# The middle stage of a two-FFN and attention layer: from three interleaved generators to slots written by hand over four rounds, with sums made by accumulating DMAs

## The chip, the cores and the metric

The kernel runs on one NeuronCore of a Trainium2 chip. A core has TensorE (PE, matrix products), VectorE (DVE), ScalarE (ACT), GpSimd (POOL) and SyncE (SP), each with an instruction queue of its own that is worked off in order, and 16 DMA engines. The metric is the device time of one execution in microseconds (us); lower is better. PEld is PE's loading of weights, which runs beside its products.

## The reference

Eight batches of 1024 tokens with 256 features pass a macaron layer: half a feed-forward network (FFN), attention, half a feed-forward network, each added to its input.

```python
x = x + 0.5 * _L0_ffn_ref(_layernorm(x), ...)
x = x + _L0_attn_ref(_layernorm(x), w_qkv, w_proj, b_proj)
x = x + 0.5 * _L0_ffn_ref(_layernorm(x), ...)
```

The FFN is a mixture of experts. A softmax over 16 expert scores per token, with a bias, picks the best two of four groups of experts and then the best two experts (`_gate`); their outputs, `silu(x We1 + be1) * (x We3 + be3)` times `We2` plus `be2`, are weighted and added. A shared FFN of width 256 is added for all tokens. The attention is linear, with 16 heads of width 16: q and k pass a ReLU, `context = sum over tokens of v k`, and the result is `context q / (q . sum of k)`, projected with `w_proj`, plus `b_proj`.

## The kernel before

Tokens lie on the 128 partitions, 8 tokens of a batch on each, so x of a batch is a tile of 128 x 8 x 256 numbers (1 MB). All numbers are fp32 but for some small masks. There are five parts in order of time.

1. *First FFN, routing* (to about 230 us). For each batch: layer norm, transposes on PE, the shared FFN (`shared_units`, L756), and `route` (L275): gate scores on PE, some 45 small DVE operations for the choice, then ranks within each expert by three small products, and 16 scatters of 128 rows each from POOL (L428), which put each token's row twice into the buffer `xs_d`, sorted by expert.
2. *First FFN, experts* (`blocks`, L573, to about 528 us): blocks of 256 rows of one expert; the results are scattered by POOL into `ys_d` (L698), two rows per token. This part's order is written out by hand (`tc.manual_schedule()`).
3. *The middle stage* (523 to 1011 us): the first FFN's expert outputs are added to x, then attention, then the second FFN's layer norm and routing. This is what changes.
4. *Second FFN, experts*: `blocks` again, to about 1288 us.
5. The shared FFN of the other batches, the expert outputs, and the stores of the result.

In the middle stage three generators run one batch apart from each other, in rounds: `begin(r)`, `attention(r - 1)` and `finish(r - 2)` (L974 to L1008). `run` (L902) takes a step of each in turn, and so writes the instructions down. The order on each engine is then made by the scheduler, which may move an instruction of one generator past those of another. What each does for its batch:

- `begin`: `combine` (L793) loads the expert outputs in eight pieces of 256 KB (SP, L798) and adds each to x on DVE (L799); `layernorm` (L209): statistics of eight 256-wide rows on DVE (L216, L217), square root on ACT (L221), two small DVE steps (L222, L224), eight scaled rows on ACT (L231); `transposed` (L238): 128 x 128 transposes on PE (L244) and copies out of PSUM on ACT (L247).
- `attention` (L805): the bias is added to x on DVE (L811); then for each of the eight token tiles j the product pk for k and q (L821), their ReLUs on ACT (L825, L826), and the product pgs of the normed x with k, added up in PSUM over all j (L829); the sum of k on DVE (L834). When all tokens are through: pks (L841), its copy ksb (L845), gsum (L848); q is scaled by its denominator on DVE (L855 to L864); the context pcx, masked to the heads (L873, L877); pm and its copy mm (L881, L882); q's transposes; and the products pp, added to x on DVE (L889, L893).
- `finish`: layer norm and transposes for the second FFN, a store of x (L983) and of the transposed x (L985) for five of the batches, and `route`. For the other three batches (5, 6, 7), x and the transposed x stay in SBUF, and their shared FFN runs as further work in the stage's last rounds. Batch 7's shared FFN of the first FFN runs in round 0.

PSUM tiles of one tag share two buffers: p1 (pk), p3 (pgs), y (pks, pm, pp) and m (all transposes, gate scores, ranks). Of the SBUF tags, x has four buffers of 1 MB, xn eight half batches, xnT six, k two.

Of the kernel before, what the change touches and what calls it, by code (L numbers as in the profile page):

```python
# [19 lines left out]
P = 128  # L20
# [6 lines left out]
def macaron_kernel(  # L27
# [108 lines left out]
    bpj = const.tile([P, D], F32, name="bpj")  # L136
    nc.sync.dma_start(out=bpj[:], in_=b_proj.partition_broadcast(P))
# [6 lines left out]
    def load_late_weights():  # L144
        for g in range(4):
            es = slice(g * E // 4, (g + 1) * E // 4)
            nc.sync.dma_start(out=wall[:, es, :], in_=wexp[:, es, :])
        nc.sync.dma_start(out=wqk_sb[:], in_=w_qkT.rearrange("(c p) f -> p c f", p=P))
        nc.sync.dma_start(out=wv_sb[:], in_=w_v.rearrange("(c p) f -> p c f", p=P))
        nc.sync.dma_start(out=wproj_sb[:], in_=w_projT.rearrange("(c p) f -> p c f", p=P))  # L150

# [56 lines left out]

    def layernorm(xt, name, res, width, parts=1):  # L209

        n = NT // parts
        for part in range(parts):
            mv = rp.tile([P, n, 2], F32, tag="mv", name=f"mv_{name}_{part}", bufs=2)
            for t in range(n):
                st = rp.tile([P, 6], F32, tag="st", name=f"st_{name}_{part}_{t}", bufs=4)
                nc.vector.bn_stats(out=st[:], in_=xt[:, part * n + t, :])  # L216
                nc.vector.bn_aggr(out=mv[:, t, :], in_=st[:])  # L217
                if t % 2:
                    yield
            rstd = rp.tile([P, n], F32, tag="rstd", name=f"rstd_{name}_{part}", bufs=2)  # L220
            nc.scalar.activation(rstd[:], mv[:, :, 1], AF.Sqrt, bias=eps_ln[:])  # L221
            nc.vector.reciprocal(rstd[:], rstd[:])  # L222
            nmr = rp.tile([P, n], F32, tag="nmr", name=f"nmr_{name}_{part}", bufs=2)
            nc.vector.scalar_tensor_tensor(  # L224
                nmr[:], mv[:, :, 0], -1.0, rstd[:], ALU.mult, ALU.mult
            )
            for i in range(n):
                h, t = divmod(part * n + i, HT)
                if t == 0:
                    res.append(half("xn", [P, HT, width], f"xn_{name}_{h}"))  # L230
                nc.scalar.activation(  # L231
                    res[h][:, t, 0:D], xt[:, part * n + i, :], AF.Identity,
                    bias=nmr[:, i : i + 1], scale=rstd[:, i : i + 1],
                )
                if t == HT - 1:
                    yield

    def transposed(xns, name, res):  # L238
        for nb, xn in enumerate(xns):
            xnT = half("xnT", [P, NC, TB], f"xnT_{name}_{nb}")  # L240
            for c in range(NC):
                pt = ps_m.tile([P, TPB, P], F32, tag="m", name=f"pt_{name}_{nb}_{c}")
                for t in range(TPB):
                    nc.tensor.transpose(  # L244
                        pt[:, t, :], xn[:, t, c * P : (c + 1) * P], ident[:]
                    )
                nc.scalar.copy(xnT[:, c, :], pt.rearrange("p t n -> p (t n)"))  # L247
            res.append(xnT)
            yield
# [25 lines left out]
    def route(base, which, b, xns, xnT, fine=False):  # L275
# [28 lines left out]
        nc.scalar.activation(pr[:], pr[:], AF.Exp)  # L304
        nc.vector.tensor_reduce(sm[:], pr[:], axis=AX.X, op=ALU.add)
# [487 lines left out]
    def combine(which, b, xt):  # L793

        for j in range(0, NT, 2):
            for k in range(K):
                y = mid.tile([P, 2, D], F32, tag="u1", name=f"y_{which}_{b}_{j}_{k}", bufs=4)
# [7 lines left out]
    def attention(b, xt, axn, axnT):  # L805
        kh, qh = [], []
        ks = mid.tile([P, NB, D], F32, tag="u3", name=f"ks_{b}", bufs=4)
        pgs = [
            ps_h.tile([P, D], F32, tag="p3", name=f"pgs_{b}_{c}") for c in range(NC)
        ]  # L810
        nc.vector.tensor_tensor(  # L811
            xt[:], xt[:], bpj[:].unsqueeze(1).to_broadcast([P, NT, D]), ALU.add
        )
        for j in range(NT):
            nb, t = divmod(j, HT)
            if t == 0:
                kh.append(half("k", [P, HT, D], f"k_{b}_{nb}"))
                qh.append(half("xn", [P, HT, D], f"q_{b}_{nb}"))
            pk = ps_h.tile([P, 2, D], F32, tag="p1", name=f"pk_{b}_{j}")
            for c in range(NC):  # L820
                nc.tensor.matmul(  # L821
                    pk.rearrange("p k d -> p (k d)"), tile_of(axnT, c, j), wqk_sb[:, c, :],
                    start=(c == 0), stop=(c == NC - 1),
                )
            nc.scalar.activation(kh[nb][:, t, :], pk[:, 1, :], AF.Relu)  # L825
            nc.scalar.activation(qh[nb][:, t, :], pk[:, 0, :], AF.Relu)  # L826

            for c in range(NC):
                nc.tensor.matmul(  # L829
                    pgs[c][:], axn[nb][:, t, c * P : (c + 1) * P], kh[nb][:, t, :],  # L830
                    start=(j == 0), stop=(j == NT - 1),
                )
            if t == HT - 1:
                nc.vector.tensor_reduce(  # L834
                    ks[:, nb, :], kh[nb].rearrange("p j d -> p d j"), axis=AX.X, op=ALU.add
                )
            yield

        pks = ps_y.tile([P, D], F32, tag="y", name=f"pks_{b}")
        for nb in range(NB):  # L840
            nc.tensor.matmul(  # L841
                pks[:], ones[:], ks[:, nb, :], start=(nb == 0), stop=(nb == NB - 1)
            )
        ksb = mid.tile([P, D], F32, tag="b2c", name=f"ksb_{b}", bufs=4)
        nc.scalar.copy(ksb[:], pks[:])  # L845
        gs = big.tile([P, NC, D], F32, tag="wc", name=f"gsum_{b}", bufs=3)
        for c in range(NC):
            nc.scalar.copy(gs[:, c, :], pgs[c][:])  # L848
        yield

        qT = []
        for nb in range(NB):
            den = rp.tile([P, HT, H], F32, tag="den", name=f"den_{b}_{nb}", bufs=1)
            qk = half("k", [P, HT, D], f"qk_{b}_{nb}")
            nc.vector.tensor_tensor(  # L855
                qk[:], qh[nb][:], ksb[:].unsqueeze(1).to_broadcast([P, HT, D]), ALU.mult
            )
            nc.vector.tensor_reduce(
                den[:], qk.rearrange("p j (h d) -> p j h d", d=HD), axis=AX.X, op=ALU.add
            )  # L860
            nc.vector.tensor_scalar(den[:], den[:], ATTN_EPS, None, ALU.add)
            nc.vector.reciprocal(den[:], den[:])
            qv = qh[nb].rearrange("p j (h d) -> p j h d", d=HD)
            nc.vector.tensor_tensor(  # L864
                qv, qv, den[:].unsqueeze(3).to_broadcast([P, HT, H, HD]), ALU.mult
            )
            yield

        cm = mid.tile([P, NC, P], F32, tag="hb", name=f"cm_{b}", bufs=3)
        for c2 in range(NC):  # L870
            pcx = ps_h.tile([P, P], F32, tag="p3", name=f"pcx_{b}_{c2}")
            for c in range(NC):
                nc.tensor.matmul(  # L873
                    pcx[:], wv_sb[:, c, c2 * P : (c2 + 1) * P],
                    gs[:, c, c2 * P : (c2 + 1) * P], start=(c == 0), stop=(c == NC - 1),
                )
            nc.vector.tensor_tensor(cm[:, c2, :], pcx[:], mask2d, ALU.mult)  # L877
# [224 lines left out]
```

## Time and profile before

| | us |
|---|---|
| median of 6 runs | 1416.37 (1411.22 to 1423.46) |
| the profiled execution | 1413.6 |
| its span, first to last instruction | 1411.9 |
| PE busy in the span | 1192.7 (84%) |
| DVE busy | 875.6 (62%) |
| ACT busy | 624.3 (44%) |
| POOL busy | 580.7 (41%) |
| the parts before the stage, 0 to 513: PE busy | 426.0 |
| the middle stage, 523 to 1011.5: PE busy | 425.1 |
| the parts behind it, 1011.5 to 1411.9: PE busy | 339.3 |

The profile is of one execution. An engine is busy while one of its instructions runs; for a group of instructions the page gives the busy time, the mean length of one, and the idle time just before them with what released it. The granted clock is the share of TensorE's full clock that it was given.

### The profile page before, as it was taken

What the parts mean: (1) busy time and instruction counts of PE and PEld (TensorE: products, weight loads), DVE (VectorE), ACT (ScalarE), POOL (GpSimd) and SP (SyncE); (2) the same over time, 40 slices, a digit from 0 to 9 for tenths busy, and PEclk for the clock granted to TensorE, in tenths of its full rate; (3) what the DMA queues carried; (4) which work ended last, traced back from release to release, by engine and by line L of the source; (5) the groups of instructions that cost most, each with busy time, mean ns of one, the idle gap of its engine ahead of it and who ended that gap; (6) DMA issues with size and microseconds to landing.
All of it is one profiled execution on the core that took longest, in us unless ns stands there. A gap on an engine that the chain in (4) does not pass through costs nothing.

```text
span 1411.9 us, 20820 instructions
## 1 busy us (share of the span) xinstructions
PE 1192.7 (84%) x5696; PEld 850.9 (60%) x5696; DVE 875.6 (62%) x2496; ACT 624.3 (44%) x1332; POOL 580.7 (41%) x688
## 2 busy tenths in 40 slices
PE   7898876977888778997977878999988889896898
PEld 3555444866777654664644645666666678773455
DVE  6787655854445537775866856738775444553666
ACT  6665322443456544464454454444344446561110
POOL 1576645566655440004044144233357665552000
PEclk9999987999999989999989999899999999998999
DMA  9344313567678876434254131010357667787896
GB/s 352 128 168 169 117 63 118 161 189 204 203 182 242 214 203 190 138 130 157 74 174 163 55 121 51 31 43 35 109 179 210 198 202 211 208 205 223 281 308 211
DMA packets 123318, 233.71 MB, mean 166 GB/s; under 512 B 20405, under 2 KB 71354, under 8 KB 118208
## 3 DMA queue, kind: packets, MB, share of 16 engines
q1 hardware_dynamic: 97664, 164.15, 40.4%
q0 software_dynamic: 25536, 68.20, 12.7%
q8 instruction: 48, 0.79, 0.2%
q14 instruction: 70, 0.57, 0.1%
HBM read 132.25 MB, written 102.64 MB: 166 GB/s over the span
## 4 chain that ended last, share of the span: by engine, by line
PE 36%; DVE 21%; issue 14%; DMA 13%; ACT 6%; POOL 5%; SPq 3%; another core or an unknown queue 2%; POOLq 0%; DVEq 0%; ACTq 0%
PE q L668 8%; PE py_s L783 5%; PE p_s L768 5%; DMA y<-ys_d 4%; POOL ys_d L698 3%; PE qy L686 3%; DMA ys_d<-yo,at 3%; PE pk L821 3%; DMA b2c<-in_be_dram 2%; PE pp L889 2%; DVE st_f L216 2%; PE pxg L647 2%; PE pt_f L244 2%; PE pgs L829 2%
## 5 line engine op out<-in xcount | busy, mean ns | idle before, releaser
L698 POOL DMA_INDIRECT ys_d<-yo,at x276 | 282.1, 1022 | 251.3 <-DVE yo L694 164.3
L668 PE MATMUL q<-xgT,wc 128*128 128x128 f32 (+1 forms) x1568 | 285.7, 333 | 59.1 <-ACT xgT L652 54.8
L428 POOL DMA_INDIRECT xs_d<-xn_f,rowi x256 | 264.8, 1034 | 107.0 <-issue 58.9
L668 PEld LDWEIGHTS q<-xgT,wc 128*128 128x128 f32 x1568 | 235.2, 199 | 83.8 <-ACT xgT L652 64.0
L691 ACT ACTIVATE yo<-qy,at 128x256 f32<-128x256 f32 x276 | 116.6, 478 | 157.2 <-PE qy L686 48.7
L768 PE MATMUL p_s<-xnT_f,ws_sb 128*128 128x512 f32 x352 | 168.5, 618 | 7.8 <-ACTq L752 6.7
L783 PE MATMUL py_s<-ws_sb,hs_s 128*128 128x256 f32 x512 | 137.0, 408 | 28.5 <-DVE hs_s L774 20.8
L694 DVE SCALAR_TENSOR_TENSOR yo<-b2c,at,yo 128x256 f32<-128x256 f32 x276 | 121.3, 478 | 63.9 <-ACT yo L691 31.8
L675 DVE SCALAR_TENSOR_TENSOR hb<-q,wc,hb 128x128 f32<-128x128 f32 (+1 forms) x196 | 73.4, 399 | 131.1 <-PE q L668 51.6
L686 PE MATMUL qy<-wall,hb 128*128 x552 | 147.4, 390 | 1.4 <-PE qy L686 0.9
L783 PEld LDWEIGHTS py_s<-ws_sb,hs_s 128*128 128x128 f32 x512 | 98.5, 202 | 74.9 <-DVE hs_s L774 35.0
L773 ACT ACTIVATE hs_s<-p_s,bc 128x512 f32<-128x512 f32 x64 | 43.8, 687 | 198.1 <-PE p_s L768 153.4
L821 PE MATMUL pk<-wqk_sb,xnT_a 128*128 128x512 f32 x256 | 128.2, 624 | 0.0
L422 POOL TENSOR_SCALAR xn_f<-cw 128x4 f32<-128x4 f32 x64 | 17.7, 283 | 252.0 <-DVE cw L394 249.1
L686 PEld LDWEIGHTS qy<-wall,hb 128*128 128x128 f32 x552 | 104.5, 198 | 16.2 <-issue 2.1
L768 PEld LDWEIGHTS p_s<-xnT_f,ws_sb 128*128 128x128 f32 x352 | 68.0, 198 | 74.0 <-issue 60.9
L647 PE MATMUL pxg<-ident,xg 128*128 128x128 f32 x552 | 87.2, 279 | 24.2 <-DMA xg<-xs_d 22.7
L652 ACT COPY xgT<-pxg 128x512 f32<-128x512 f32 x138 | 82.2, 596 | 57.3 <-PE pxg L647 32.7
L674 ACT ACTIVATE hb<-q,wc 128x128 f32<-128x128 f32 (+1 forms) x196 | 76.3, 426 | 63.9 <-PE q L668 28.8
L647 PEld LDWEIGHTS pxg<-ident,xg 128*128 128x128 f32 x552 | 68.8, 144 | 45.3 <-DMA xg<-xs_d 14.9
L799 DVE TENSOR_TENSOR x<-x,y 128x512 f32<-128x512 f32 x104 | 69.1, 685 | 40.6 <-DMA y<-ys_d 23.3
L829 PE MATMUL pgs<-k,xn_a 128*128 128x256 f32 x256 | 69.8, 391 | 11.8 <-issue 8.8
(292 smaller groups left out, 1709.7 us busy)
## 6 DMA issues: line engine op xcount, KB each, us to landing
y<-ys_d SPq DMA_DIRECT2D x128, 256.0 KB
b2c<-in_be_dram SPq DMA_DIRECT2D x196, 128.0 KB
xg<-xs_d SPq DMA_DIRECT2D x80, 264.0 KB
xg<-xs_d SPq DMA_DIRECT2D x116, 132.0 KB
x<-xk SPq DMA_DIRECT2D x10, 1024.0 KB
xk<-x SPq DMA_DIRECT2D x9, 1024.0 KB
out_dram<-x SPq DMA_DIRECT2D x7, 1024.0 KB
wall<-in_wexp_dram SPq DMA_DIRECT2D x4, 1540.0 KB
```

Of the source, the lines that this page charges most:

```text
L428: nc.gpsimd.indirect_dma_start(out=v[:, :], out_offset=bass.IndirectOffsetOnAxis(ap=rowi[:, j, k : k + 1], axis=0), in_=xn[:, t, :], in_of ...
L647: nc.tensor.transpose(pt[:, c, s * P : (s + 1) * P], xg[i][:, s, c * P : (c + 1) * P], ident[:],)
L652: nc.scalar.copy(xgT[i][:], pt[:])
L668: nc.tensor.matmul(pt_[:, cs], w[:, s, o + c * P : o + (c + 1) * P], t[:, c, cs], start=(c == 0), stop=(c == NC - 1),)
L686: nc.tensor.matmul(py[:, s : s + 1, :], h[:, s * P : (s + 1) * P], w2s[s % len(w2s)], start=True, stop=True,)
L691: nc.scalar.activation(yo[:, s, :], py[:, s, :], AF.Copy, scale=a[:, s, 1:2])
L694: nc.vector.scalar_tensor_tensor(yo[:, s, :], b2[:, s % b2.shape[1], :], a[:, s, 1:2], yo[:, s, :], ALU.mult, ALU.add,)
L698: nc.gpsimd.indirect_dma_start(out=ys_views[i * NR + s][:, :], out_offset=bass.IndirectOffsetOnAxis(ap=a[:, s, 0:1].bitcast(I32), axis=0), ...
L768: nc.tensor.matmul(pt[:], w[:, c, s * P : (s + 1) * P], xnT[nb][:, c, :], start=(c == 0), stop=(c == NC - 1),)
L783: nc.tensor.matmul(py[:, t - t0, :], hs[s][:, t * P : (t + 1) * P], ws2_sb[:, s, :], start=(s == 0), stop=(s == NS - 1),)
L821: nc.tensor.matmul(pk.rearrange("p k d -> p (k d)"), tile_of(axnT, c, j), wqk_sb[:, c, :], start=(c == 0), stop=(c == NC - 1),)
L829: nc.tensor.matmul(pgs[c][:], axn[nb][:, t, c * P : (c + 1) * P], kh[nb][:, t, :], start=(j == 0), stop=(j == NT - 1),)
```

## The change

The first and last two parts stay as they are, but for a bias: `b_proj` is no longer kept in SBUF, but written eight times in a row into a buffer in DRAM, `bpj_d`, at the start.

In the middle stage:

- `combine` no longer adds the first FFN's expert outputs. `add_outputs` issues, from POOL, DMAs that add the outputs in DRAM to x in SBUF (`accum_op`), 1 MB each, two per batch; for batch 0 in two halves. `add_rows` adds the bias in the same way. (The last part of the kernel still uses `combine`.)
- The order of the stage is written by hand (`tc.manual_schedule()`): eleven rounds of eight slots, in which four batches are in work at once. In round r, batch g = r gets its first layer norm (slots 3 to 7), a = r - 1 the products over its tokens (one j per slot), p = r - 2 the rest of its attention (slots 0 to 6), and f = r - 3 the second layer norm's rows, transposes and the start of its routing (slots 0 to 3).
- The routing's further steps are spread by a table (`PLAN`; `SOON` for batch 6, `PART` for batch 7) over the slots up to slot 6 of the next round. `route` now gives way after the exponential too, and after each scatter.
- `layernorm`, `transposed` and `attention` become classes and functions whose pieces can be called one by one. q is kept in four tiles of two token tiles each, in other buffers (tags u1 and u3), and its scaling works on these 512-wide tiles in place of 1024-wide ones. qk uses tag u2 and not k, and pcx tag y and not p3.
- The shared FFN of batches 5 and 6 takes one step per slot in rounds 9 and 10 (rounds 8 and 9 before), batch 7's follows alone, as before. Round 0 is filled in the same way.

```diff
-    bpj = const.tile([P, D], F32, name="bpj")
-    nc.sync.dma_start(out=bpj[:], in_=b_proj.partition_broadcast(P))
+    bpj_d = tc.dram_tile([NT, D], F32, name="bpj_d")
...
+        nc.sync.dma_start(out=bpj_d[:, :], in_=b_proj.partition_broadcast(NT))
...
+    class Norm:
+        def stats(self, t):
+            st = rp.tile([P, 6], F32, tag="st", name=f"st_{self.name}_{t}", bufs=4)
+            nc.vector.bn_stats(out=st[:], in_=self.xt[:, self.first + t, :])
+            nc.vector.bn_aggr(out=self.mv[:, t, :], in_=st[:])
+        def scale(self):
...
+            nc.scalar.activation(self.rstd[:], mv[:, :, 1], AF.Sqrt, bias=eps_ln[:])
+            nc.vector.reciprocal(self.rstd[:], self.rstd[:])
...
+        def row(self, i):
...
+            nc.scalar.activation(
+                self.rows_[h][:, t, 0:D], self.xt[:, self.first + i, :], AF.Identity,
+                bias=self.nmr[:, i : i + 1], scale=self.rstd[:, i : i + 1],
+            )
...
         nc.scalar.activation(pr[:], pr[:], AF.Exp)
+        if fine:
+            yield
...
+    def add_outputs(b, xt, parts=1):
+        n = NT // parts
+        for k in range(K):
+            for i in range(parts):
+                js = slice(i * n, (i + 1) * n)
+                nc.gpsimd.dma_start(
+                    out=xt[:, js, :], in_=ys_v[k, b, :, js, :], accum_op=ALU.add
+                )
+    def add_rows(xt, src):
+        nc.gpsimd.dma_start(
+            out=xt.rearrange("p j d -> p (j d)"),
+            in_=src.rearrange("j d -> (j d)").partition_broadcast(P), accum_op=ALU.add,
+        )
...
+        def scale_q(self, nb):
...
+            for i, q in enumerate(pairs):
+                qk = mid.tile([P, 2, D], F32, tag="u2", name=f"qk_{b}_{nb}_{i}", bufs=3)
+                nc.vector.tensor_tensor(
+                    qk[:], q[:], self.ksb[:].unsqueeze(1).to_broadcast([P, 2, D]), ALU.mult
+                )
...
-    for r in range(B + 2):
-        if 2 <= r + 1 < B - 1:
-            xs[r + 1] = load_x(r + 1, xk_d[r + 1])
-        s = r - 3
-        run(
-            finish(r - 2) if r >= 2 else None,
-            attention(r - 1, xs[r - 1], *axns.pop(r - 1)) if 1 <= r <= B else None,
-            begin(r) if r < B else None,
-            late if r == 0 else None,
-            shared_units(xs[s], xnTs.pop(s), f"s1_{s}") if s >= B - LATE else None,
-        )
...
+    PLAN = {0: 1, 2: 2, 3: 2, 4: 1, 5: 1, 6: 1, 7: 1, 8: 4, 9: 4, 10: 4, 11: 4}
+    SOON = {0: 1, 1: 2, 2: 2, 3: 2, 5: 2, 6: 4, 7: 4, 8: 4, 9: 4}
+    PART = {0: 1, 1: 1, 2: 1}
...
+    def plan(r, b):
+        steps = PART if b == B - 1 else SOON if b == B - 2 else PLAN
+        for o, n in steps.items():
+            planned.setdefault((r + (3 + o) // 8, (3 + o) % 8), []).append((b, n))
...
+    def slot(r, s):
+        g, a, p, f = r, r - 1, r - 2, r - 3
+        G, A, Q, F = (0 <= b < B for b in (g, a, p, f))
+        if A:
+            att[a].products(s)
+            if s > 0:
+                att[a].over_tokens(s - 1)
+        if s == 0:
+            if Q:
+                att[p].over_tokens(NT - 1)
+                att[p].sum_k(1)
+                att[p].sums()
+            if A:
+                turn_half(axn[a], 1, f"a{a}", axnT[a])
+                add_rows(xs[a], bpj_d)
+            if F:
+                norm_f[f].stats(6)
+                norm_f[f].stats(7)
+                norm_f[f].scale()
+                norm_f[f].row(0)
+                norm_f[f].row(1)
+                if f < B - LATE:
+                    nc.sync.dma_start(out=xk_d[f][:], in_=xs[f][:])
+        elif s == 1:
+            if Q:
+                att[p].context()
...
+            if Q:
+                att[p].scale_q(0)
+            if F:
+                turn_half(xns[f], 0, f"f1_{f}", xnTs[f])
+        elif s == 2:
+            if Q:
+                att[p].project()
...
+            if Q:
+                att[p].scale_q(1)
+                att[p].turn_q(0)
+            if F:
+                turn_half(xns[f], 1, f"f1_{f}", xnTs[f])
+        elif s == 3:
+            if F:
...
+                routes[f] = route(base, 1, f, xns.pop(f), xnTs[f], True)
+                plan(r, f)
+            if Q:
+                att[p].turn_q(1)
+            if 2 <= r + 1 < B:
+                xs[r + 1] = load_x(r + 1, xk_d[r + 1])
+            if G:
+                norm_a[g] = Norm(xs[g], 0, NT, f"a{g}", axn.setdefault(g, []), D)
+                for t in range(4):
+                    norm_a[g].stats(t)
+            if Q:
+                att[p].add(0)
+        elif s == 4:
...
+            if A:
+                att[a].sum_k(0)
...
+            if Q:
+                att[p].add(2)
+            if 2 <= r + 1 < B:
+                add_outputs(r + 1, xs[r + 1])
+        elif s == 5:
+            if Q:
+                att[p].add(4)
+            if G:
+                norm_a[g].stats(6)
+                norm_a[g].stats(7)
+                norm_a[g].scale()
...
+        elif s == 6:
+            if Q:
+                att[p].add(6)
+            if G:
+                for i in range(4):
+                    norm_a[g].row(i)
...
+        elif s == 7:
+            if G:
+                for i in range(4, 8):
+                    norm_a[g].row(i)
+                axnT[g] = []
+                turn_half(axn[g], 0, f"a{g}", axnT[g])
...
+        for b, n in planned.pop((r, s), ()):
+            steps_of(routes[b], n)
+        if (r, s) == (B + 2, 3):
+            first.extend(first_map(base, 1))
+    with tc.manual_schedule():
+        add_outputs(0, xs[0], 2)
+        add_outputs(1, xs[1])
+        for r in range(B + 3):
...
+            for i in range(8):
+                slot(r, i)
+                if filler is not None:
+                    next(filler, None)
```

## The prediction, on record before the changed kernel ran

> **What bounds the kernel now.** I read the page's 40 slices first (35.3 us each; the middle stage is slices 16 to 29, counted from 1), then the middle stage cut at the starts of its rounds, then that stage's waits and groups, and last single instructions in order of time.
>
> ```profile
> PE   7898876977888778997977878999988889896898
> DVE  6787655854445537775866856738775444553666
> PEclk9999987999999989999989999899999999998999
> ```
>
> TensorE (PE) is the fullest engine in the stage, VectorE (DVE) second; in slices 21 to 25 PE stands at 7 or 8 tenths and DVE at 5 to 8, so neither is full there. The cut gives the size (columns: stretch, length, busy time of each engine, granted clock, DMA share, GB/s):
>
> ```profile
> 523.00:557.50 34.50, 28.96 (x74) 15.54 (x75) 22.19 (x52) 10.56 (x17) 4.34 (x5) 0.82 0.54 169
> ...
> 713.00:767.00 54.00, 43.52 (x202) 28.95 (x201) 37.61 (x103) 25.49 (x59) 18.20 (x26) 0.91 0.42 141
> ...
> 949.50:1011.50 62.00, 59.02 (x253) 36.94 (x254) 46.22 (x121) 24.27 (x38) 20.57 (x24) 1.00 0.17 55
> 523.00:1011.50 488.50, 425.09 (x1835) 274.60 (x1836) 335.94 (x854) 218.18 (x463) 132.77 (x174) 0.94 0.31 104
> ```
>
> The stage takes 488.5 us, PE is busy for 425.1 of them, and **63.4 us of PE idle time is all that a new order can win**. About 41 of it lies between 659 and 871: a full round there takes 54 us and PE works 43.5. The end (949.5 on) is nearly full already. Those holes are chains through in-order queues (waiter, what it waited for, total, times, longest; 505 to 1010 us):
>
> ```profile
> DVE rstd_a L222 <- ACT rstd_a L221: 27.4, 6, 7.1
> DVE x L799 <- DMA x<-xk: 17.0, 4, 8.2
> DVE ks L834 <- ACT k L825: 15.9, 3, 7.5
> ```
>
> One hole, as instructions (start, length, engine, line, idle before and its releaser):
>
> ```profile
> 759.44 0.59 PE L841 MATMUL pks<-ks,ones 128*128 128x256 f32 x2
> 764.62 2.17 PE L244 MATMUL pt_f<-ident,xn_f 128*128 128x128 f32 x8 [4.58 <-issue]
> ```
>
> PE stands for 4.58 us until the last batch's sums on DVE, square root and rows on ScalarE (ACT) are through: every batch ends in such a tail, and little else is ready.
>
> **Part 1: the outputs and the bias leave DVE.** Groups of the stage:
>
> ```profile
> L799 DVE TENSOR_TENSOR x<-x,y 128x512 f32<-128x512 f32 x48 | 31.7, 683 | 20.2 <-DMA x<-xk 17.0 <-DMA y<-ys_d 3.1
> L811 DVE TENSOR_TENSOR x<-x,bpj 128x2048 f32<-128x2048 f32 x6 | 13.7, 2278 | 0.0
> ```
>
> Eight adds of 0.68 and one of 2.28 go per batch: 7.7 us of DVE's 37.6 per round. The hand order gives some back: the query scaling becomes six 512-wide operations for three 1024-wide, twice (about 0.2 us each pair more), and routing steps now stand one behind the other, each on the one before (0.33 us from start to start at 752, against 0.20 when mixed with others). I put DVE at 33 us a round: no bound, but long chains.
>
> In their place POOL issues three accumulating DMAs per batch (four halves for batch 0): about 1 us each by the scatters' 1.03 (L428), so 3 more on its 18 of 54. The second add of a tile waits for the first to land, and the first for the load of x; behind them on POOL stand 12 scatters of the routing, and who waits for those is only the ring of eight xn tiles, two rounds later. Hidden in a full round: the load is issued in slot 3, x is wanted one round later. SP loses 64 loads of y, at which it stood for up to 20.3 us waiting for DVE (L798, the queue's own waits); the loads of x behind them go sooner, and the 17.0 us of DVE waits on them shown above go.
>
> The trace has no accumulating DMA. Low end: a plain load of x, issued 768.30, used 774.74: 6.4 us per MB. High end: that row doubled, 12.8, since the add reads x too. I take 8: the best slice of this trace's DMA moves 381 GB/s, 2.75 us per MB, doubled is 5.5, and 2.4 for landing (a scatter at 978.22 took 2.44). [...]
>
> **Part 2: the rounds.** PE's work is unchanged. Per batch, from start to start in the rows (two records per matmul): pk 32 x 0.43 = 13.8; pgs and pp 32 x 0.215 = 6.9 each; three sets of transposes 3.45 each = 10.4; pks, pcx, pm 0.86 each = 2.6; gate and ranks 1.9. Sum 42.5. A shared unit: 32 x 0.43 + 32 x 0.215 = 20.6. 8 x 42.5 + 4 x 20.6 = 422, against 425.1 busy. What the new order adds is where PE waits in a full round. I followed the four queues by hand from the end of the third product pair (pp of j=4, slot 5; call it 0):
>
> - *pk of slot 0.* ACT must pass: add and two statistics on DVE 1.7, root 0.3, reciprocal, next statistics and the softmax's start on DVE 2.1, exponential 0.3, then k/q 0.66, four rows 2.0, k/q 0.66, four rows 2.0, two copies 1.05: 10.8. PE has pg 0.4, two pk, two pgs, pp and transposes until then: 9.0. **Wait 1.8 to 2.3.**
> - *pks, slot 0.* DVE after the exponential (4.75): softmax 0.8, add 0.6, statistics 1.1, scores and groups 3.3, statistics 1.1, first pick 1.95, sum of k 1.9: done at 15.5. PE is there at 14.0 to 14.5. **Wait 1 to 1.5.**
> - *first transposes of xn_f, slot 1.* After pks, ACT: copies 0.6, table load 1.28, root 0.3, DVE 0.5, rows and k/q 2.7: 5.4 behind the transposes of slot 0; PE has 3.5. **Wait 1.5 to 1.9.**
> - *second transposes of xn_f, slot 2.* Both PSUM buffers of tag m are in use until ACT has copied the queries: **0.6**.
>
> 5.5 us, and about 0.1 for each of a dozen hand-overs: **6.8. Full round 42.5 + 6.8 = 49.3**, against 54.
>
> **Sum of the stage** (PE work plus waits):
> - round 0: the shared unit runs from 523. y can be read at 530.3 (the last scatter of the blocks lands); issue 1, data 5.5 for each add, one landing 2.4: both adds end near 544.5; statistics, root, rows, transposes and copy 7.5 more: pk starts at 551.5, against 557.5. **28.5**
> - round 1: 23.3 + 2.7 = **26**; round 2 with the context phase: 37.2 + 2.8 = **40**; round 3, without an older routing: **47**; rounds 4 to 7: 4 x 49.3 = **197**
> - round 8: 40.8 + 4.2 = **45**; round 9, shared unit 5 as filler: 39.8 + 3.2 = **43**; round 10, unit 6 and the block list on DVE (some 8 us, partly covered): 26 + 4 = **30**; the last unit alone: 20.6 + 2.4 = **23**
>
> 479.5 against 488.5: 9 less. So the gain per full round (4 to 5 us, five times) is mostly spent on a pipeline that is one stage deeper and on a last unit without company, which stood among other work in the old end. The stages before and after keep their instructions and order. The profiled execution took 1413.6 (span 1411.9 and 1.7 around it): 1413.6 - 9 = 1404.6, I say **1405**. The median of the runs shown is 1416.4, 2.8 above that execution; I keep the execution's base and leave the 2.8 to the range. The measurement can tell about 0.5%, 7 us, from no change.
>
> **The rivals.**
> - *The full round is tighter.* If pp of j=4 ends while DVE is already through its older work, as it is in my walk, small shifts pay: with the softmax's steps 2 us earlier the first two waits go, and 44 a round is left: 5 x 5 us less, **1380**. For it: 917 to 949.5 ran with 0.2 us of PE idle. Against: that stretch had an independent shared unit as filler, a full round has none.
> - *The full round is as long as the old ones.* Waits that my walk doesn't have come on top, as the ACT wait at 776.83 (3.31 us, releaser unknown to the profile), and in a hand order nothing else may step in: 52 a round, 5 x 2.7 = 13 more, **1418**. Then the change only shifts idle time.
> - *Slower: the accumulating DMA costs 12.8 us per MB.* Place: rounds 0 to 2, where it isn't hidden. Batch 0's two adds end near 557, pk starts at 564.5 (+13); batch 1's end at 583 where 575 is wanted (+8); the bias add and batch 2's end at 621 where 615 is wanted (+6): 1405 + 27 = **1432**. In later rounds 3 x 12.8 = 38 still fits in 49. It makes the kernel slower by over 0.5% from about 11 us per MB.
> - *It doesn't do what it says*: the built order has the slots as written on every queue, so I give this nothing.
>
> **How the numbers follow.** Forecast (1397 to 1411) 0.38; tighter rounds (1374 to 1396) 0.22; as long as before (1412 to 1421) 0.16; slow accumulation (1422 to 1436) 0.18; beyond either end 0.06. The range 1376 to 1434 takes in both ends of the DMA's price. Faster by over 0.5% (under 1407 to 1409): 0.28 of the forecast's 0.38, all of the tighter case and 0.02 beyond: 0.52. Same: 0.10 of the forecast, 0.13 of the third case: 0.23. Slower: the rest of it 0.03, the slow accumulation 0.18, 0.04 beyond: 0.25.
>
> **What would show it.** pk of batch 0 starting near 551 (DMA price); pk of successive batches 49 us apart in rounds 4 to 7, against 54; PE idle in front of pk of slot 0, pks and pt_f, released by ACT xnT_a, DVE ks, ACT xn_f; no DVE wait on DMA in rounds 3 to 7; the three POOL DMAs landing well ahead of the statistics. Wrong if PE's longest waits stand elsewhere (a POOL or SP queue), if a full round exceeds 52 or is under 46, or if the end, rounds 9 and 10 and the last unit, takes more than 100 us.

## The result and the profile after

The changed kernel takes 1437.3 us (median of 20 runs, 1425.5 to 1451.6), the kernel before 1413.1 (46 runs). The ratio is **1.016, 95% interval 1.014 to 1.018**: 1.6% slower, where 1405 and "faster" had been forecast. The ratios, and the medians in the table further down, leave out runs more than 1.5% above the fastest of their kernel: three of the changed kernel's here, one of e5_after's six, and one of e6_sched_only's four, which took 6550 us for a reason that stays unknown. The profiled execution of the changed kernel took 1442.3, its span is 1440.6. In later groups of runs the ratio was 1.033 (1.027 to 1.039) on a chip on which the kernel before takes 1325, and 1.014 (1.010 to 1.019) on one on which it takes 1426. So below, where nothing else is said, only runs of one group, on one chip, are compared with each other.

The page's 40 slices for the changed kernel (36.0 us each; the stage is slices 15 to 29):

```profile
PE   7999776987888778898887987886797888897998
```

PE isn't fuller than before in the full rounds, and slices 26 to 29, all 9 at the old end, are 8, 8, 6 and 7. The stage cut by time (stretch, length, busy time of PE, PEld, DVE, ACT and POOL, granted clock, DMA share, GB/s): the start, one full round, and the whole stage.

```profile
527.70:565.20 37.50, 27.40 (x73) 15.89 (x74) 12.00 (x29) 11.55 (x19) 10.18 (x11) 0.79 0.79 161
...
723.89:775.24 51.35, 42.51 (x199) 28.28 (x198) 35.60 (x101) 24.75 (x55) 20.84 (x29) 0.93 0.64 166
...
527.70:1041.50 513.80, 429.06 (x1823) 276.94 (x1824) 317.43 (x835) 218.82 (x465) 155.05 (x200) 0.91 0.47 121
```

The stage takes 513.8 us, against 488.5, and PE is idle for 84.7 of them, against 63.4. The profiled execution is 28.7 us longer in all: the last scatter of the first experts comes 4.7 later (532.65 against 527.97, in code that the change doesn't touch), from there to the first product of the second experts it is 508.9 against 484.5, 24.3 more, and the rest of the kernel is 399 in both.

The long waits on DVE for the root and for x went, as meant, and new ones came (505 to 1040 us; waiter, waited for, total, times, longest):

```profile
DVE x L966 <- PE pp L962: 46.8, 16, 6.6
...
PE pk L866 <- ACT xnT_a L264: 13.7, 7, 2.4
...
PE pxg L673 <- DMA xg<-xs_d: 12.9, 3, 11.0
...
PE pt_q L263 <- ACT xnT_q L264: 11.0, 6, 2.0
...
PE pks L900 <- DVE ks L888: 10.7, 4, 6.3
...
DVE st_a L220 <- DMA xf<-ys_d: 6.3, 2, 5.7
...
DVE rstd_a L227 <- ACT rstd_a L226: 5.9, 8, 3.0
```

DVE's wait for the root (rstd_a) fell from 27.4 to 5.9, and its 17.0 for loads of x became 6.3 for the accumulating DMAs, both at the start. But PE now waits for small things in a fixed order, and 11.0 us once for pxg, the first transposes of the second experts; and DVE waits 46.8 us for the products pp, for which it waited 14.9 before. What such waits look like in a full round, as instructions (start, length, engine, line, idle before and its releaser):

```profile
769.13 1.98 PE L866 MATMUL pk<-wqk_sb,xnT_a 128*128 128x512 f32 x4 [2.11 <-ACT xnT_a L264]
...
774.50 0.70 PE L900 MATMUL pks<-ks,ones 128*128 128x256 f32 x2 [2.09 <-DVE ks L888]
775.04 1.21 PE L263 MATMUL pt_a<-ident,xn_a 128*128 128x128 f32 x8
776.05 3.44 PE L866 MATMUL pk<-wqk_sb,xnT_a 128*128 128x512 f32 x4
...
788.86 0.66 PE L263 MATMUL pt_q<-ident,q 128*128 128x128 f32 x4 [1.56 <-ACT xnT_q L264]
790.19 1.12 PE L263 MATMUL pt_f<-ident,xn_f 128*128 128x128 f32 x4 [0.68 <-ACT xnT_q L264]
792.04 1.12 PE L263 MATMUL pt_f<-ident,xn_f 128*128 128x128 f32 x4 [0.73 <-ACT xnT_f L264]
792.95 3.52 PE L866 MATMUL pk<-wqk_sb,xnT_a 128*128 128x512 f32 x4
```

The four products of a pk take 1.88 to 1.98 us as a rule, and 3.44 and 3.52 at 776 and 793. The granted clock shows why: it is halved there. Four pieces of the same round, as in the table above (PE's busy time is the first figure behind the length, the clock the third from the end):

```profile
772.36:775.77 3.41, 1.32 (x10) 1.17 (x10) 3.10 (x6) 0.50 (x3) 2.60 (x3) 1.00 0.33 119
775.77:779.18 3.41, 3.41 (x7) 1.61 (x6) 0.59 (x4) 2.88 (x5) 1.55 (x3) 0.50 0.63 114
...
786.01:789.42 3.41, 1.75 (x11) 0.86 (x9) 3.34 (x6) 2.69 (x6) 0.00 (x0) 1.00 0.00 0
789.42:796.25 6.83, 5.42 (x13) 2.98 (x13) 6.33 (x20) 1.76 (x3) 1.33 (x3) 0.50 0.93 303
```

In this stage the clock is halved for 3.41 us or a multiple of it (6.8, 10.2 and once 17.0 us), each time behind 3.41 us in which PE worked little. Cut into such pieces, the stage has 12 at full clock with PE busy for less than 43% of the time, and half clock followed all of them; it followed 5 of 13 pieces with 43 to 64%, and none of 99 with more. So **a wait costs itself, and where waits fill much of such a piece, products at half speed as well**; the pk at 769.13, right behind a wait of 2.11, is not slow. In this round no single wait is longer than 2.11 us, and yet the clock is halved twice, for 3.41 and 6.83 us. From the last scatter of the first experts on, 25 whole pieces of the stage are at half clock, 85.3 us; in the kernel before it was 16, 54.6 us.

### The profile page after: what moved, and what is told of

It reads as the page before. It is cut to its first block, busy times and chain, and to the rows that moved or that the text cites. A ratio compares the mean times of both kernels' runs of the same rounds, so it can differ in the third digit from the quotient of the medians.

```text
span 1440.6 us, 20660 instructions
## 1 busy us (share of the span) xinstructions
PE 1198.2 (83%) x5696; PEld 850.3 (59%) x5696; DVE 859.0 (60%) x2472; ACT 624.3 (43%) x1331; POOL 604.1 (42%) x714
## 5 line engine op out<-in xcount | busy, mean ns | idle before, releaser
L694 PEld LDWEIGHTS q<-xgT,wc 128*128 128x128 f32 x1568 | 234.2, 199 | 81.0 <-ACT xgT L678 45.4
L809 PE MATMUL py_s<-ws_sb,hs_s 128*128 128x256 f32 x512 | 141.7, 418 | 30.6 <-DVE hs_s L800 26.5
L866 PE MATMUL pk<-wqk_sb,xnT_a 128*128 128x512 f32 x256 | 139.7, 673 | 13.7 <-ACT xnT_a L264 13.7
L809 PEld LDWEIGHTS py_s<-ws_sb,hs_s 128*128 128x128 f32 x512 | 101.6, 208 | 77.9 <-DVE hs_s L800 43.0
L799 ACT ACTIVATE hs_s<-p_s,bc 128x512 f32<-128x512 f32 x64 | 43.7, 687 | 204.0 <-PE p_s L794 175.1
L673 PEld LDWEIGHTS pxg<-ident,xg 128*128 128x128 f32 x552 | 67.6, 144 | 71.5 <-issue 31.6
L866 PEld LDWEIGHTS pk<-wqk_sb,xnT_a 128*128 128x128 f32 x256 | 51.1, 214 | 54.8 <-issue 36.5
L794 PE MATMUL p_s<-xnTr,ws_sb 128*128 128x512 f32 x160 | 74.6, 609 | 6.2 <-issue 3.4
```

The costliest lines, as they stand in the source:

```text
L673: nc.tensor.transpose(pt[:, c, s * P : (s + 1) * P], xg[i][:, s, c * P : (c + 1) * P], ident[:],)
L694: nc.tensor.matmul(pt_[:, cs], w[:, s, o + c * P : o + (c + 1) * P], t[:, c, cs], start=(c == 0), stop=(c == NC - 1),)
L794: nc.tensor.matmul(pt[:], w[:, c, s * P : (s + 1) * P], xnT[nb][:, c, :], start=(c == 0), stop=(c == NC - 1),)
L809: nc.tensor.matmul(py[:, t - t0, :], hs[s][:, t * P : (t + 1) * P], ws2_sb[:, s, :], start=(s == 0), stop=(s == NS - 1),)
L866: nc.tensor.matmul(pk.rearrange("p k d -> p (k d)"), tile_of(self.axnT, c, j), wqk_sb[:, c, :], start=(c == 0), stop=(c == NC - 1),)
```

## The experiments

All are timed against the kernel before; the ratio is that of the runs, with its 95% interval. Group 1 ran where the kernel before takes 1327.2 us, group 2 where it takes 1426.2, group 3 where it takes 1324.9. Theory A: the loss is at the seam between the stage and the experts. Theory B: it is the accumulating DMAs. Theory C: it is the order by hand itself.

| run | what | us | ratio |
|---|---|---|---|
| group 1: e1_seam | barrier put back | 1363.4 | 1.028 (1.023 to 1.033) |
| e2_seam_fill | and shared units earlier | 1357.6 | 1.023 (1.019 to 1.027) |
| e3_seam_dve | barrier, sums on DVE | 1393.7 | 1.048 (1.043 to 1.052) |
| e4_seam_sched | barrier, order by the scheduler | 1282.9 | 0.966 (0.962 to 0.970) |
| group 2: e5_after | the changed kernel | 1448.0 | 1.014 (1.010 to 1.019) |
| e6_sched_only | order by the scheduler | 1371.3 | 0.960 (0.956 to 0.964) |
| e7_hand_shift | barrier, order by hand with three shifts | 1415.2 | 0.990 (0.987 to 0.994) |
| e8_sched_dve | barrier, scheduler, sums on DVE | 1379.4 | 0.969 (0.964 to 0.974) |
| group 3: e9_after | the changed kernel | 1368.2 | 1.033 (1.027 to 1.039) |
| e10_seam | barrier put back | 1362.2 | 1.031 (1.026 to 1.037) |
| e11_before_accum | kernel before, sums by accumulating DMAs | 1342.3 | 1.013 (1.008 to 1.017) |
| e12_sched_shift | barrier, scheduler, three shifts | 1278.1 | 0.967 (0.962 to 0.972) |

### The seam

The kernel before has a barrier (`tc.no_sync_barrier()`) between the stage and the second experts; the change drops it. PE's first transposes of the experts (pxg) then stand in PE's order in the middle of round 10, ahead of the second products of batch 6's shared unit and of the whole shared unit of batch 7.

```diff
         run(shared_units(xs[s], xnTs.pop(s), f"s1_{s}"))
+    tc.no_sync_barrier()
     last = first + [routes[B - 1]]
```

Expected of e1_seam:

> The changed kernel with the barrier between the middle stage and the second experts put back: the first expert transposes (pxg) stand behind the last shared unit again. Theory A (the seam: PE stands 12.7 us at those transposes, since batch 6's scatters are late, while a whole shared unit is queued behind them) expects 10 to 13 us less than the changed kernel's 1437, so 1424 to 1427, and the first product of the experts near 1030 where it was 1041.5. Theory B (the accumulating DMAs at the start and in the rounds) and theory C (the rounds written by hand) expect the time that the seam's stall leaves to be spent waiting for the same scatters further on: under 4 us gained, 1433 or more.

That names a time of another chip, so the run was repeated beside the changed kernel. Expected of that pair:

> The changed kernel as it is once more, as the partner on the same chip of the run with the barrier alone: 1.014 to 1.016 on a chip where the kernel before takes 1410 to 1430, more on a faster one.

> The barrier alone, beside the changed kernel on the same chip. Theory A: 10 to 13 us (0.7 to 0.9 per cent) under it, since PE's 12.7 us in front of the experts' first transposes go. The rival: within 4 us of it, since the last shared unit then waits or runs alone all the same.

In group 3 the barrier is worth 6.0 us (1368.2 to 1362.2), and the intervals of the two overlap: less than theory A's 10 to 13, and not clear of the rival's "within 4". The traces say why it isn't more. The end of round 10 in e9_after, and then in e10_seam (PE's instructions, as above):

```profile
957.98 1.09 PE L673 MATMUL pxg<-ident,xg 128*128 128x128 f32 x4 [11.09 <-DMA xg<-xs_d]
960.66 1.09 PE L673 MATMUL pxg<-ident,xg 128*128 128x128 f32 x4 [1.59 <-DMA xg<-xs_d]
```

```profile
947.11 1.22 PE L809 MATMUL py_s<-ws_sb,hs_s 128*128 128x256 f32 x2 [6.26 <-DVE hs_s L800]
```

Without the barrier PE stands 12.7 us at pxg, since the rows of batch 6 are not scattered yet. With it that wait is gone, but PE stands 6.26 us at the same place for hs_s: on DVE the block list of the experts (`first_map`, 23 instructions from 931.47 to 942.73 in e10_seam) stands in one piece ahead of the shared unit's steps. The longer wait had covered the shorter one. From batch 7's ksb to the experts' first product it is 113.8 us without the barrier and 111.4 with it.

For more company in the last rounds, e2_seam_fill begins each shared unit in slot 3 of the batch's own round (their second product uses PSUM tag m):

```diff
-            filler = late if r == 0 else None
-            if r in late_ffn:
...
+                if i == 3 and r - 3 >= B - LATE:
+                    s = r - 3
+                    fillers.append(shared_units(xs[s], xnTs.pop(s), f"s1_{s}", (ps_m, "m")))
+                if fillers and next(fillers[0], StopIteration) is StopIteration:
+                    fillers.pop(0)
```

> As the run before, and the shared units of batches 5, 6 and 7 begin in slot 3 of rounds 8, 9 and 10, as soon as their transposed x is there, where they began in slot 0 of rounds 9 and 10 and after round 10 (their second product uses PSUM tag m, since tag p3 is held by the sums over tokens in round 8). Theory A in its wider form (the end of the stage has 36 us more idle time on PE than the old end, half of it from the seam, half from work without company in rounds 8 to 10) expects 8 to 12 us below the run before, near 1415. If only the barrier mattered: no more than 3 below it. If the routing of batch 6 sets the end (its scatters landed at 1010, the first expert product can't come before some 1014 to 1016): the first product near 1016 and PE idle in front of it.

It gained 5.8 us against e1_seam, with intervals that overlap, and not 8 to 12. The two edits at the end are worth some 12 us together, where the changed kernel loses 43 on a chip like this one (1324.9 to 1368.2 in group 3). So the end by itself doesn't hold the loss.

### The order by hand

One edit to the changed kernel, e6_sched_only (and with the barrier e4_seam_sched): the slots are written down as they are, but the scheduler may move the instructions on each engine.

```diff
-    with tc.manual_schedule():
+    if True:
         add_outputs(0, xs[0], 2)
```

> As the first run, but the order written by hand is only the order in which the instructions are written down; the scheduler may move them on each engine, as in the kernel before. Theory C (the fixed order makes the rounds 51 where 49 was forecast) expects full rounds under 49 and 10 us or more gained against the first run. The rival (the fixed order is worth what it costs) expects rounds of 51 to 55 and the same time or up to 20 us more.

> The changed kernel with one edit: its slots are still written down in the same order, but the scheduler may move the instructions on each engine. No barrier at the end of the stage. The run with the barrier gave 0.966 of the kernel before. Theory C (the fixed order is nearly the whole loss) expects 0.96 to 0.975 here too; theory A expects that without the barrier at least 10 us of that are lost, 0.975 or more.

**Theory C holds, and far beyond its own size.** With the barrier the edit takes 80.5 us off (1363.4 to 1282.9, where 10 or more were expected), and rounds 4 to 8 take 37 to 44. In group 2 the edit alone takes 76.6 us off (1447.95 to 1371.32); the kernel with it is 4% faster than the one before, and so beats both. The stage in e6_sched_only (first line: rounds 5 to 8; second: from the last scatter to the first product of the experts)

```profile
709.05:880.98 171.93, 151.10 (x770) 105.27 (x769) 121.30 (x375) 91.57 (x207) 83.67 (x107) 0.97 0.52 146
...
534.60:971.40 436.80, 393.81 (x1832) 264.53 (x1830) 282.70 (x833) 215.42 (x463) 155.54 (x197) 0.96 0.52 135
```

and in e5_after, on the same chip (the whole first, then rounds 5 to 8):

```profile
529.30:1042.00 512.70, 429.25 (x1829) 278.18 (x1828) 316.57 (x832) 218.33 (x463) 152.82 (x197) 0.91 0.46 118
...
719.20:927.60 208.40, 173.91 (x777) 114.70 (x776) 138.19 (x384) 93.83 (x208) 80.02 (x107) 0.89 0.44 119
```

The same 1830 products: 75.9 us less in the stage, of which 40.5 are idle time of PE (83.5 to 43.0) and 35.4 are busy time (429.3 to 393.8). Most of the second part can be the clock, 0.96 granted in place of 0.91: it is at half for 34.1 us in place of 85.3, and products at half speed cost up to half of that difference, 25.6 us. What the other 9.8 are stays open. DVE's busy time falls too, from 316.6 to 282.7, for the same instructions. One reason, its instructions in e6_sched_only show:

```profile
748.60 0.27 DVE L282 TENSOR_TENSOR oh<-sc,mx_2a 128x128 f32<-128x128 f32 x1
748.79 0.17 DVE L221 BATCH_NORM_AGGREGATE mv_a<-st_a 128x2 f32<-128x6 f32 x1
748.88 0.39 DVE L220 BATCH_NORM_STATS2 st_a<-x 128x6 f32<-128x256 f32 x1
749.19 0.27 DVE L285 TENSOR_TENSOR oh<-oh,rev 128x128 f32<-128x128 f32 x1
```

and in e5_after, two routing steps and the statistics of two rows:

```profile
774.13 0.29 DVE L285 TENSOR_TENSOR oh<-oh,rev 128x128 f32<-128x128 f32 x1
774.46 0.29 DVE L288 TENSOR_REDUCE mx_2b<-oh 128x8 f32<-128x128 f32 x1
...
789.16 0.40 DVE L220 BATCH_NORM_STATS2 st_a<-x 128x6 f32<-128x256 f32 x1
...
789.69 0.40 DVE L220 BATCH_NORM_STATS2 st_a<-x 128x6 f32<-128x256 f32 x1
```

The scheduler lays the routing's steps between the statistics' steps, so that an instruction doesn't follow the one that it depends on: one pair of statistics and one routing step together take 0.59 us (748.60 to 749.19). In the order by hand the two kinds stand in blocks, 0.53 for a pair of statistics and 0.33 for a routing step, 0.86 in all. How much of the 33.9 us comes from this was not counted.

Could the order by hand be mended? e7_hand_shift puts the barrier back and moves three pieces, each against a wait of the full round above (condensed; rows 5 to 7 stood ahead of `scale_q(1)`):

```diff
 slot 0:  att[p].sum_k(1)
-         att[p].sums()
          turn_half(axn[a], 1, f"a{a}", axnT[a])
+         att[p].sums()
...
 slot 2:  att[p].scale_q(1); att[p].turn_q(0)
-         turn_half(xns[f], 1, f"f1_{f}", xnTs[f])
+         for i in (5, 6, 7): norm_f[f].row(i)
 slot 3:
+         turn_half(xns[f], 1, f"f1_{f}", xnTs[f])
...
 slot 7:
-         for i in range(4, 8): norm_a[g].row(i)
          turn_half(axn[g], 0, f"a{g}", axnT[g])
+         for i in range(4, 8): norm_a[g].row(i)
```

Expected of e5_after, the changed kernel once more as this group's base, and of e7_hand_shift:

> The changed kernel as it is, beside the kernel before on the chip of this call, as the base of the other runs (the runs so far were on a chip on which the kernel before takes 1327 and not 1413). Theory A expects a ratio of 1.035 or more on a chip like that, so that the barrier alone (1.028 there) is worth 10 us; if the ratio is near 1.028, the barrier is worth nothing.

> The order stays by hand, with the barrier, and three pieces of it are shifted against the waits seen in a full round: in slot 7 the transposes of the first half of axn go ahead of rows 4 to 7 on ACT (PE waits 2.1 there), in slot 0 the transposes of the second half go ahead of pks (2.1), and the second transposes of the second norm move from slot 2 to slot 3 behind a pair of products, with rows 5 to 7 behind the copies of q (1.6 + 0.7 + 0.7). If each of these waits costs its length and also a cold clock (four-product groups pk of 3.4 to 3.6 us right behind a wait, 1.88 otherwise, so 1.5 to 1.7 each), 7 us of waiting and about 5 of slow products go: full rounds of 40 to 45, 35 to 60 us less in all than the run with the barrier alone (1.028). If the waits only move to the next instruction, as in-order queues may do: rounds of 48 to 51 and less than 15 us gained. If the loss is elsewhere than in this order (DMA, POOL): no change.

The first can't be told: on this chip the kernel before took 1426, and not 1327. e7_hand_shift is 32.8 us faster than the changed kernel (1447.95 to 1415.20), some 27 without the barrier's share (6.0 in group 3): under the 35 to 60 expected, and over the rival's 15. Rounds 4 to 6 take 45.5, 46.5 and 45.4 us, a little over the 40 to 45, for 49.4, 50.8 and 51.4 in e5_after. Rounds 5 to 8 and the whole stage:

```profile
722.04:909.96 187.92, 160.01 (x769) 107.89 (x768) 138.00 (x384) 92.79 (x206) 82.66 (x109) 0.96 0.50 134
...
539.00:1016.60 477.60, 414.09 (x1834) 270.91 (x1834) 316.58 (x829) 217.92 (x464) 151.19 (x197) 0.95 0.49 125
```

Again both fall, PE's busy time by 13.9 and its idle time by 6.6 in the four rounds. Of the 75.9 us between the two orders the three shifts and the barrier explain 35.1; the other 40.8 are spread over the whole stage (136.9 for 151.7 in rounds 1 to 4, 171.9 for 187.9 in rounds 5 to 8, 90.4 for 106.6 at the end, and 6 back at the start). The largest wait left in the four rounds is pks for the sum of k on DVE (9.7 us in 2 waits); what the rest is made of stays open.

The same shifts under the scheduler, e12_sched_shift:

> The three shifts of the order by hand, with the barrier, but under the scheduler. If the scheduler had already found what the shifts bring: 0.955 to 0.97, as without them. If they add to it: under 0.955. If the written order decides less than the priorities that it sets, and the shifts delay the second norm: 0.97 to 0.985.

0.967 (0.962 to 0.972) against 0.966 (0.962 to 0.970) without them in group 1: no difference. Under the scheduler the shifts bring nothing more.

### The accumulating DMAs

With the order by hand, e3_seam_dve puts the sums back on DVE:

```diff
-        add_outputs(0, xs[0], 2)
-        add_outputs(1, xs[1])
+        sums[0] = sums_by_step(0, xs[0])
...
+        if s >= 4 and r + 1 in sums:
+            next(sums[r + 1])
```

`sums_by_step` is `combine` with its y in tag u2; the bias add stands on DVE in slot 4.

> As the first run, but the first FFN's outputs are loaded in 256 KB pieces and added on DVE, step by step in slots 4 to 7 of the round before (batch 0: slots 0 to 3 of round 0), and the bias is added on DVE: no accumulating DMA, the order by hand kept. Theory B expects a gain of 8 us or more against the first run, most of it at the start: pk of batch 0 near 556 in place of 565. Theory C and A expect 0 to 10 us more than the first run, since DVE gets 7.7 us per round in its chains and a full round of 51 grows to 52 to 54.

30.2 us slower than e1_seam: theory B is wrong, and the others' 0 to 10 was too little. Rounds 5 and 6 take 54.2 and 54.8 us, in e1_seam 51.3 and 50.6. The 7.0 us more in the two are PE's wait in front of pks for the sum of k on DVE, 9.3 us in place of 2.4: the further DVE instructions stand in a fixed row ahead of something that PE waits for. pk of batch 0 starts 39.9 after the last scatter, against 31.4 in e1_seam, so even at the start these DMAs are no loss against the adds in this order.

Under the scheduler, e8_sched_dve:

> Scheduler and barrier as in the 0.966 run, but the first FFN's outputs and the bias are added on DVE, with no accumulating DMA. If the accumulating DMAs are a gain where they are hidden (7.7 us of DVE per batch): 10 to 50 us more than 0.966 of the kernel before, 0.975 to 1.00. If they cost (at the start, where the DMA engines move some 200 GB/s at full load against 390 for plain loads): 0 to 10 us less, 0.96 or under.

0.969 against 0.960: 8.1 us more in the medians, with the barrier as a further difference, and close to e4_seam_sched's 0.966, which has the barrier but ran elsewhere. That lies between the two expectations: the DMAs are worth a few microseconds there, if anything. And alone, in the kernel before (condensed):

```diff
-        yield from combine(0, b, xs[b])
+        for k in range(K):
+            nc.gpsimd.dma_start(out=xs[b][:, js, :], in_=ys_v[k, b, :, js, :], accum_op=ALU.add)
...
-        nc.vector.tensor_tensor(xt[:], xt[:], bpj[:].unsqueeze(1).to_broadcast([P, NT, D]), ALU.add)
+        nc.gpsimd.dma_start(out=xt.rearrange("p j d -> p (j d)"),
+            in_=bpj_d.rearrange("j d -> (j d)").partition_broadcast(P), accum_op=ALU.add)
```

> The kernel before, its generators and its scheduled order, with the first FFN's outputs and the bias added by accumulating DMAs: the other part of the change alone. With the slots under the scheduler these DMAs were worth 0.009 (0.960 against 0.969). If they are worth the same here: 0.98 to 0.995. If the slots are needed to hide them (the load of x, two adds one after the other and the bias add stand in a chain of some 30 us in front of a batch): 1.00 to 1.03.

1.013: 17.4 us slower, in the range of the second expectation. In its stage PE's transposes wait 25.9 us (5 times) for ACT's copies of the transposed second norm, and ACT's rows 18.8 us (5 times) for the routing's scatters, two waits that the kernel before has not, while POOL, which also issues the scatters, stands 48.0 us (twice) at adds for a load of x. That fits adds in the way of scatters on POOL; no run tests it. So the two parts of the change aren't a sum. The DMAs lose 17 us in the old generators, gain 30 in the slots by hand, and change little in the slots under the scheduler. What the other parts of the change do alone (the tags, the narrower scaling of q) was not run.

## Why the prediction failed

*The forecast of the stage against the changed kernel's trace* (from one start of a round's ksb to the next): round 0, 28.5 forecast and 37.5 measured; round 1, 26 and 26.9; round 2, 40 and 38.4; round 3, 47 and 43.7; rounds 4 to 7, 197 and 203.4; round 8, 45 and 51.1; rounds 9, 10 and the last unit, 96 and 112.9. Together 479.5 and 513.8. The terms that failed most are the end (+17) and the start (+9); rounds 4 to 7 together and round 8 are +6 each.

- **"... the built order has the slots as written on every queue, so I give this nothing"** is the first step that failed, twice. The order has PE's pxg in the middle of round 10, by which the end lost 12.7 us of waiting (the forecast's own sign, more than 100 us for rounds 9, 10 and the last unit, came true: 112.9). "The stages before and after keep their instructions and order" left out that the barrier was gone. And where the slots do stand as written, that was taken as no price. It is more than the whole loss: the same slots cost 76.6 us less if the scheduler may move them, where the changed kernel loses 22 on that chip.
- **"63.4 us of PE idle time is all that a new order can win"** is the second. An order can win busy time too: e6_sched_only spends 27 us less of it than the kernel before did in its profile (393.8 against 420.6, from the last scatter on), besides less idle time. Half clock explains up to 10 of them (34.1 us of it against 54.6).
- **"Three sets of transposes 3.45 each"** is a wrong size. A set has 16 records in the kernel before (128 for eight batches), and eight of them take 0.88 us from start to start where no wait stands ahead:

```profile
L244 PE MATMUL pt_a<-ident,xn_a 128*128 128x128 f32 x128 | 23.3, 315 | 4.8 <-ACT xnT_a L247 3.8 <-ACT xn_a L231 0.9
...
711.62 2.17 PE L244 MATMUL pt_f<-ident,xn_f 128*128 128x128 f32 x8 [4.51 <-issue]
...
736.13 1.04 PE L244 MATMUL pt_q<-ident,q 128*128 128x128 f32 x8
737.01 1.03 PE L829 MATMUL pgs<-k,xn_a 128*128 128x256 f32 x4
```

  So a set takes 1.8, three sets 5.3 in place of 10.4, and a round's work is 37.4 and not 42.5. The 3.45 is twice a set, as "two records per matmul" would give; rows at half clock, like the first one shown (granted clock 0.50, behind a wait of 4.51 us), are as dear, so the working alone doesn't tell which it was. The cross-check (422 by the rows against 425 busy) agreed by accident, since records too many stood against a busy time that holds products at half speed.
- *The full round*, 49.3 forecast, 49.7 to 51.6 measured, was near by luck: 42.5 + 6.8 by the forecast; by the trace, on the mean of rounds 4 to 7 (50.9), 37.4 of products at full speed, 6.2 of further busy time and 7.3 of waits. The waits' sum was about right. Their places were right for pk (2.1 to 2.4 in each round), but pks waits 2.1 in one round and 0.4 in the others, and the first transposes of the second norm 1.0 at most, for 1.5 to 1.9. The second ones with tag m, and the last ones of q with them, cost 3.0 to 3.4 us (1.56 + 0.68 + 0.73 in the round shown) and not 0.6.
- *The accumulating DMA* was priced well: 8 us per MB taken, 8.3 to 8.4 measured from one issue to the next that waits for it, while little else ran (POOL, changed kernel); beside other transfers one took 15.5 (588.62 to 604.10), and no DVE instruction waited for it.

```profile
576.32 0.87 POOL L837 DMA_DIRECT2D x<-ys_d  x1 [13.71 <-issue]
584.74 0.86 POOL L837 DMA_DIRECT2D x<-ys_d  x1 [7.56 <-DMA x<-ys_d]
```

  While such DMAs kept the DMA engines busy (some 540 to 555 us), they moved about 200 GB/s, against up to 395 in the plain loads and the store issued at 566 us. About half the rate shows here, then, and the doubling in the forecast was the author's estimate; but the price is 8.3 and not the 12.8 that came of doubling the whole load. The slow rival's 1432 lies near the result by luck: its mechanism isn't what cost the time.
- *The start*: of the 9 us, 2 are the second pair of adds, which ran beside batch 1's and landed at 551.2; the other 7 are batch 0's chain from there to pk at 565.2, 14 us in place of 7, as DVE, ACT and PE work it in the written order between the pieces of the shared unit. (The scheduler doesn't make the start shorter: 37.6 us from the last scatter to pk in e6_sched_only, 31.6 in e5_after.) The 4.7 us by which the whole stage began later come on top.
- *Tighter round, 44 us*: rated at 0.22 for the order by hand, whose rounds never were that short. Under the scheduler it was too careful: rounds 4 to 8 of e4_seam_sched take 37 to 44.
- *"Hidden in a full round"* and *"no DVE wait on DMA in rounds 3 to 7"* held: DVE's 6.3 us of waiting for these DMAs all lie in round 0.

## What to carry to other kernels

Before an order is fixed by hand, run the same program text once with the scheduler left on: here the new stages and the fixed order came in one change, the first (slots, DMAs and tags together) worth 55 us and the second a loss of 77. Take an engine's work from rows that have no wait in front of them, since on TensorE the same eight transposes took 2.17 us behind a wait, at a granted clock of 0.50, and 1.04 without one, at 1.00; count the records of a group; and add to the waits the products at half clock that can follow: in the stage above they came behind all 12 full-clock pieces of 3.41 us in which PE was busy for less than 43%, and behind 5 of 13 with 43 to 64%. When a stall is taken away, look for the second engine that is late at the same place: the 12.7 us in front of pxg hid 6.3 of another wait.

## What was not expected of the hardware

- TensorE's clock was halved without a single long wait. In the full round shown, waits of 2.1 us at most, which left PE busy for 1.32 or 1.75 of 3.41 us, were followed by 3.41 or 6.83 us at half clock (pk 3.44 and 3.52 us there for four records, 1.88 to 1.98 else). Between two orders of the same products that made 51 us of difference in time at half clock, up to 25.6 us of busy time.
- The same code ran 6 to 8% faster on one chip than on another (1325 and 1413 to 1426 us for the kernel before). In the changed kernel and its variants much of the difference lay in the parts with many transfers: the first experts took 250.6 us with 219 GB/s in e1_seam and 272.7 with 201 GB/s in the first profile of the changed kernel; rounds 5 to 8 took 204.4 and 204.7. So the ratio of two kernels moved with the chip, from 1.014 to 1.033; why the chips differ stays open.
- In the stage, dependent DVE instructions that followed each other cost more than when another chain's instruction stood between them (0.86 us in blocks in e5_after and 0.59 mixed in e6_sched_only, for the same three); the stage's DVE busy time fell from 316.6 to 282.7 us by order alone, of which this is a part.
